# Four graph layers on one core: later small steps, a shorter split, tail products moved forward, last norms without a square root

## Chip, cores, metric

The kernel runs on one core of a Trainium2 chip. The metric is the device time of one execution in microseconds (us). The engines are TensorE (PE), VectorE (DVE), ScalarE (ACT), GpSimd (POOL) and SyncE (SP, here the queue that issues nearly all DMAs).

## The reference, cut to what matters

A graph of 3125 nodes with 128 features and 103125 edges, sorted by target, passes four layers; each is added to its input and layer-normalized over the features:

```python
x = _layernorm(x + L0(x, src, dst, edge_weight, W, b))  # relu(sum of w * (x@W)[dst] into src, + b)
x = _layernorm(x + L1(x, [src, dst], ...))   # 4-head GAT: softmax of leaky_relu(a_s[src] + a_d[dst]),
                                             # weighted sum, + bias + x@skip_W + skip_b, own layer norm
x = _layernorm(x + L2(x, Wq, Wk, Wv, Wo))    # edge attention: x + softmax(q.k) V @ Wo
x = _layernorm(x + L3(x, ...))               # two SAGE layers (mean of neighbours), sigmoid
```

## The kernel before

Nodes are padded to 3200: 25 blocks of 128. The kernel never gathers edges one by one after the front. **The front** builds two dense 3200 x 3200 matrices in DRAM from one-hot products: `f_ctd` (edge counts, bf16) and `wd` (summed edge weights, f32). All later sums are matrix products against blocks of them. PE, DVE and ACT work from instruction streams that are fixed at build time; the order in each stream is that of the program as a scheduler settles it, and a waiting instruction holds all behind it on its engine.

**Layer 0.** `add0(pool, i, accs, blocks)` loads row block `i` of `wd` (tile `cw`, line 790, on SP) and multiplies it into accumulators in PSUM (line 794). The first 20 target blocks (`Z0`) have the five banks `acc0`; their `add0` calls run inside the loop of the front as rows are written, the last two after it, with `cw` in the pool `f_zp` of three buffers. The last five blocks (`acc1`, tiles `left`) come in a second loop over all 25 row blocks: the **tail**. Between its calls stand `marks`: `scores1(g)` (transposes `turned` L909 and attention products L1087, L1091), `top`, `factors`, `values`. `end0` does relu, residual and layer norm of one bank (L801, L762 to L773).

**Layer 1** runs over `items`: four groups of target blocks (`IG`: 4, 7, 7, 7 blocks), two head pairs and 25 source blocks `c`. In each step `masks` loads a count block (`ct`, L1213) and makes two 0/1 masks, on ACT and DVE (L1225, L1226) or on DVE alone (L1219); `products` multiplies counts and masks with `vp` (L1236, L1241). `values(b)` fills `vp` for two blocks: it scales, splits f32 into three bf16 pieces (`split3`, L549 to L555) and writes a negated copy of one part (L1144). It is called four steps ahead within the first 25 steps.

All small work is put between steps with `later(k, f)`: `f` runs `k` steps on. `skips` makes the skip product of one block (L1249, read by L1250); `quotients`, then `finish1` with `first_norm`, `first_scale`, `second_norm`, `second_scale` end a group; `turns` then takes each block through `turn2`: `one` transposes (L984), `two` multiplies by `wyv` (L988), read by ACT (L989) and DVE (L990). `bound2` finds the largest norm (`highest` L942, `spread` L953). All of these write PSUM through `bank()`:

```python
    def bank():
        return spare[-1]()
        spare.append(lambda: zps.tile([P, 512], F32, name="few", tag="acc1"))   # tail, group 0
                spare.append(lambda: ap.tile([P, 512], F32, name="few"))        # groups 1 to 3
        spare.append(lambda: ss.tile([P, 512], F32, name="s"))                  # layer 2
```

In groups 1 to 3 seven of the eight banks are accumulators, and the eighth is the only one for small work.

**Layer 2** runs over two groups of targets (13 and 12 blocks) and 25 source blocks: scores (L1373), exponential (L1376), times counts (L1377), products (L1381). The first steps also hold the end of layer 1's last group, and `degrees` (a transpose L1354, ACT copy `rt` L1356, two DMAs). `finish2` normalizes: the first group in two halves between steps (`norm1`, `norm2`), the second at once by `layer_norm` with the scaling on DVE (L778).

**Layer 3** multiplies the counts with three-piece splits (`in_parts`) of its input (L1476) and of the hidden layer (L1549). At the end each of seven groups passes: sums (L1565), sigmoid on ACT (L1568), residual (L1569), `layer_norm` with square root (L767) and scaling (L773) on ACT, output DMA on SP (L1573, L1577).

## Time and profile before

| | |
|---|---|
| median of 3 runs | 1536.65 us (1534.05 to 1539.7) |
| profiled execution: time, span | 1536.56 us, 1534.5 us |
| mean PE clock granted, 1 = full | 0.979 |
| layer 1's products, first and last (L1236, L1241) | 547.8 to 961.2 us |
| layer 3's first product, PE's last product | 1261.65, 1516.07 us |
| last output DMA issued | 1528.1 us |

"L1249" is line 1249 of the kernel. A wait reads: waiting engine and line <- engine and line that released it. Busy PE is modelled from the instruction's size, so a full PE row says that PE had work, not that it ran at its peak.

### The profile page before, as it was taken

How to read it: one execution, taken by the hardware profiler on the slowest of the kernel's cores; microseconds unless marked ns; L12 is line 12 of the kernel's file. 1: busy time of each engine (PE TensorE's matmuls, PEld its weight loads, DVE VectorE, ACT ScalarE, POOL GpSimd, SP SyncE). 2: the span in 40 equal slices, each digit the busy share in tenths (PEclk: the TensorE clock that was granted, in tenths of full speed). 3: DMA queues.
4: the chain of work that ended last, by engine and by line, in shares of the span. 5: the costliest groups of instructions: out<-in, count | busy, mean ns of one | idle time of the engine just before them, and what ended most of it. 6: DMA issues, size and time to landing. Idle time of an engine off the chain costs nothing.

```text
span 1534.5 us, 35155 instructions
## 1 busy us (share of the span) xinstructions
PE 1400.5 (91%) x14871; PEld 1223.6 (80%) x14871; DVE 981.0 (64%) x1574; ACT 923.4 (60%) x1880; POOL 122.5 (8%) x136
## 2 busy tenths in 40 slices
PE   4899999999997978899989989899999989999995
PEld 3898999998997867899979889577777764458995
DVE  4999899989991389778878887544464360012005
ACT  2988778888882489878778676544474340023006
POOL 1000000000000023203311320300000000000000
PEclk9999999999999999999999999999999999999998
DMA  6387787878877623444434333332222226513551
GB/s 192 91 220 207 203 234 206 235 202 223 214 214 232 222 85 101 143 118 125 132 115 134 114 87 95 106 94 68 67 72 73 82 105 238 193 44 129 195 195 45
DMA packets 210368, 224.39 MB, mean 146 GB/s; under 512 B 72892, under 2 KB 184007, under 8 KB 209945
## 3 DMA queue, kind: packets, MB, share of 16 engines
q1 hardware_dynamic: 206344, 217.74, 48.4%
q10 hardware_dynamic: 3457, 2.35, 0.6%
q8 instruction: 118, 1.93, 0.5%
q0 software_dynamic: 400, 1.97, 0.4%
q14 instruction: 49, 0.40, 0.1%
HBM read 157.67 MB, written 64.36 MB: 145 GB/s over the span
## 4 chain that ended last, share of the span: by engine, by line
PE 40%; DVE 5%; ACT 2%; issue 1%; POOL 1%; DMA 1%; DVEq 0%; ACTq 0%; SPq 0%; POOLq 0%
PE acc L1381 9%; PE s L1373 8%; PE acc L1476 7%; PE acc L1549 6%; PE acc L1241 4%; PE acc L1236 2%; DVE cm L1226 1%; DVE nz L1260 1%; PE tr L1513 1%; PE acc L1513 1%; DMA ct<-f_ctd 1%; ACT fm L1225 1%; DVE cm L1219 0%; PE tr L1505 0%; PE acc L1505 0%
## 5 line engine op out<-in xcount | busy, mean ns | idle before, releaser
L1241 PE MATMUL acc<-vp,cm 128*128 128x198 bf16 x2500 | 344.7, 252 | 6.6 <-DVE cm L1226 4.1
L1225 ACT ACTIVATE fm<-adr,bas 128x896 bf16<-128x896 f32 (+1 forms) x320 | 286.5, 952 | 68.0 <-DVE cm L1226 63.1
L1236 PE MATMUL acc<-vp,ct 128*128 128x204 bf16 x1250 | 315.2, 256 | 10.0 <-DVE vp L1144 5.6
L1241 PEld LDWEIGHTS <-cm 128*128 128x128 bf16 x2500 | 236.0, 98 | 26.5 <-issue 10.6
L872 PE MATMUL wp<-wod,ohc 128*128 128x128 bf16 x3840 | 244.0, 219 | 8.8 <-ACT cs L877 6.6
L872 PEld LDWEIGHTS <-ohc 128*128 128x128 bf16 x3840 | 224.0, 98 | 9.8 <-issue 9.4
L833 DVE TENSOR_TENSOR wod<-ohd,w 128x4096 bf16<-128x4096 bf16 (+1 forms) x120 | 225.0, 1931 | 0.6 <-PE wp L872 0.6
L1226 DVE TENSOR_TENSOR cm<-fm,ct 128x896 bf16<-128x896 bf16 (+1 forms) x320 | 198.1, 649 | 36.1 <-PE acc L1241 14.1
L842 ACT ACTIVATE wod<-ohd,wu 128x128 bf16<-128x128 bf16 x640 | 197.0, 400 | 0.0
L1377 DVE TENSOR_TENSOR e<-e,ct 128x416 f32<-128x416 f32 (+1 forms) x175 | 110.4, 636 | 108.2 <-ACT e L1376 102.6
L1376 ACT ACTIVATE e<-s,f_nm 128x416 f32<-128x416 f32 (+1 forms) x175 | 111.5, 642 | 99.4 <-PE s L1373 94.1
L1381 PEld LDWEIGHTS acc<-self__8127,e 128*128 128x128 f32 x1250 | 148.4, 193 | 21.5 <-issue 19.7
L1373 PE MATMUL s<-yT,f_xT 128*128 128x416 f32 (+1 forms) x350 | 145.8, 552 | 4.6 <-ACT rt L1356 4.0
L1381 PE MATMUL acc<-self__8127,e 128*128 128x129 f32 x1250 | 148.7, 276 | 0.6 <-DVE e L1377 0.6
L794 PE MATMUL acc<-f_xw,cw 128*128 128x128 f32 x1000 | 118.4, 278 | 7.4 <-DMA cw<-wd 7.4
L1236 PEld LDWEIGHTS <-ct 128*128 128x128 bf16 x1250 | 122.4, 98 | 2.5 <-issue 1.5
L883 ACT COPY ws<-wp 128x512 f32<-128x512 f32 x160 | 93.6, 585 | 49.8 <-PE wp L872 48.2
L794 PEld LDWEIGHTS acc<-f_xw,cw 128*128 128x128 f32 x1000 | 115.0, 194 | 7.6 <-DMA cw<-wd 7.6
L864 PE MATMUL cp<-ohc,ohd 128*128 128x125 bf16 x1280 | 96.7, 218 | 21.1 <-ACT ws L883 17.9
L1373 PEld LDWEIGHTS s<-yT,f_xT 128*128 128x128 f32 x350 | 62.2, 191 | 57.7 <-issue 40.6
L1476 PE MATMUL acc<-ct,ip 128*128 128x512 bf16 (+1 forms) x525 | 104.9, 360 | 1.4 <-DMA ct<-f_ctd 1.4
L1549 PE MATMUL acc<-ip,ct 128*128 128x128 bf16 x1875 | 105.2, 219 | 0.0
(277 smaller groups left out, 1482.7 us busy)
## 6 DMA issues: line engine op xcount, KB each, us to landing
ct<-f_ctd SPq DMA_DIRECT2D x50, 800.0 KB
wd<-ws SPq DMA_DIRECT2D x40, 896.0 KB
ct<-f_ctd SPq DMA_DIRECT2D x150, 224.0 KB
cw<-wd SPq DMA_DIRECT2D x50, 640.0 KB
f_ctd<-cs SPq DMA_DIRECT2D x20, 1000.0 KB
ct<-f_ctd SPq DMA_DIRECT2D x25, 416.0 KB
ct<-f_ctd SPq DMA_DIRECT2D x25, 384.0 KB
cw<-wd SPq DMA_DIRECT2D x25, 320.0 KB
```

Of the source, the lines that this page charges most:

```text
L794: nc.tensor.matmul(accs[j // 4][:, j % 4, :], cw[:, j - h, :], xw[:, i, :], start=False, stop=(i == NB - 1 and (j % 4 == 3 or j == n - 1)) ...
L833: nc.vector.tensor_tensor(f[:, 0:n].rearrange("p w (a t) -> p w a t", t=2), ohd[:, 0:n].rearrange("p w (a t) -> p w a t", t=2), twos(w2[s] ...
L842: nc.scalar.activation(wod[2][:, BW + w, :], ohd[:, BW + w, :], AF.Copy, scale=w3[:, 1, at : at + 1])
L872: nc.tensor.matmul(wp[:, j, :], ohc[:, w, :], wod[s][:, w, :], start=(j == 0 and q == 0 and s == 0), stop=(j == 3 and q == 1 and s == 2), ...
L1225: nc.scalar.activation(f[:, : n * P], at, AF.Relu, bias=bas[:, c, h : h + 1], scale=UP)
L1226: nc.vector.tensor_tensor(m[:, : n * P], f[:, : n * P], ct[:, : n * P], OP.min)
L1236: nc.tensor.matmul(out_(F1, PW), ct[:, k * P : (k + 1) * P], vp[:, c, hp : hp + 2, :, 2 * F1 : V1], start=(c == 0), stop=False, skip_group ...
L1241: nc.tensor.matmul(out_(0, 2 * F1)[:, j], ms[j][:, k * P : (k + 1) * P], vp[:, c, hp + j, :, 0 : 2 * F1], start=False, stop=(c == NB - 1 a ...
L1373: nc.tensor.matmul(s[:, :m], xT[:, c * P : (c + 1) * P], yT[:, i0 * P + a : i0 * P + a + m], start=True, stop=True)
L1381: nc.tensor.matmul(acc[k // 3][:, (k % 3) * (P + 1) : (k % 3 + 1) * (P + 1)], es[q, c][:, k * P : (k + 1) * P], vo[:, c, 0 : P + 1], start ...
L1476: nc.tensor.matmul(acc[k][:, :n], ips[b // 4][:, b % 4, s, :], ct[:, c : c + n], start=(b == 0 and s == 0), stop=(b == NB - 1 and s == 2),)
L1549: nc.tensor.matmul(acc[g][:, j, :], ct[:, (b0 + j) * P : (b0 + j + 1) * P], ups[b // 4][:, b % 4, s, :], start=(b == 0 and s == 0 and j == ...
```

## The change

- `split3` writes the third piece straight from the second subtraction: an f32 tile and an ACT copy less in each split.
- `layer_norm` gets an engine for the scaling (`by`) and, with `bits`, an inverse square root from the number's bits and three Newton steps on DVE. Without `by` ACT scales, as most callers had it.
- The PSUM pool of the front closes sooner, and twelve of the 25 tail calls run ahead of the last two calls on `acc0`, six before each. `marks` come one call earlier.
- `values` negates with one POOL instruction instead of one DVE instruction per block.
- `bank(n)` takes a width. In the tail and group 0 two banks alternate; in groups 1 to 3 one tile is kept, in three slices. `turn2` takes a slice for each of its steps.
- Skips every second step instead of every step; quotients after 8 steps instead of 4; the gaps of `finish1` grow; the bound's rest comes 2 steps later.
- `degrees` at step 7 of layer 2; the second group of layer 2 is normalized in halves, with ACT scaling; layer 3's transposes and sum of degrees come a few blocks later.
- At the end POOL scales the first five groups; the last two take the Newton norm and DVE.

```diff
@@ split3
-        u = pool.tile(room or shape, F32, name=name + "2")[:, 0 : shape[1]]
-        nc.vector.tensor_tensor(u, t, o(1), OP.subtract)
-        nc.scalar.copy(o(2), u)
+        nc.vector.tensor_tensor(o(2), t, o(1), OP.subtract)
@@ layer_norm(lp, o, i, blocks, by=None, bits=False)
+        if bits:
+            v = lp.tile([P, n], F32, name="var")
+            nc.vector.tensor_scalar(v, mv[:, :, 1], EPS, None, OP.add)
+            k = lp.tile([P, n], I32, name="half")
+            nc.vector.tensor_scalar(k, v.bitcast(I32), 1, None, OP.arith_shift_right)
+            nc.vector.tensor_scalar(sd.bitcast(I32), k, -1.0, float(0x5F3759DF), OP.mult, OP.add)
+            t = lp.tile([P, n], F32, name="newton")
+            for _ in range(3):
+                nc.vector.tensor_tensor(t, sd, sd, OP.mult)
+                nc.vector.scalar_tensor_tensor(t, t, -0.5, v, OP.mult, OP.mult)
+                nc.vector.scalar_tensor_tensor(sd, t, 1.5, sd, OP.add, OP.mult)
+        else:
+            nc.vector.tensor_scalar(sd, mv[:, :, 1], EPS, None, OP.add)
+            nc.scalar.activation(sd, sd, AF.Sqrt)
+            nc.vector.reciprocal(sd, sd)
+        if by:
+            for b in range(n):
+                by.tensor_scalar(
+                    o[:, b0 + b, :], i[:, b0 + b, :], mv[:, b, 0:1], sd[:, b : b + 1], OP.subtract, OP.mult
+                )
+            return
...
@@ after the loop of the front
+    fps.close()
+    zpp = zero.enter_context(tc.tile_pool(name="f_zpp", bufs=1, space=PSUM))
...
+    early = 0
     for i in range(done, NB):
+        for _ in range(6):
+            add0(zp, early, acc1, (Z0, NB - Z0))
+            early += 1
         add0(zp, i, acc0, (0, Z0))
@@ turn2
-        t = bank()
         def one():
+            t = bank(P)
...
         def two():
-            nc.tensor.matmul(t[:, P : 3 * P], xT[:, b * P : (b + 1) * P], wyv, start=True, stop=True)
+            t = bank(2 * P)
+            nc.tensor.matmul(t[:, 0 : 2 * P], xT[:, b * P : (b + 1) * P], wyv, start=True, stop=True)
@@ bound2
-        later(1, rest)
+        later(2, rest)
@@ finish1
-            later(gap[0], lambda: turns(0))
+            later(2 * gap[0] - 1, lambda: turns(0))
...
-                later(1, two)
+                later(gap[2], two)
                 later(2, lambda: turns(j + 1))
...
-                        later(1, lambda q=q: bound2(sp, q))
+                        later(gap[2], lambda q=q: bound2(sp, q))
@@ values
-            for k in range(n):
-                nc.vector.tensor_scalar(
-                    vp[:, b + k, :, :, 2 * F1 : 3 * F1], vp[:, b + k, :, :, F1 : 2 * F1], -1.0, None, OP.mult
-                )
+            both_ = vp[:, b : b + n].rearrange("p b h s c -> p b (h s) c")
+            nc.gpsimd.tensor_scalar(both_[:, :, :, 2 * F1 : 3 * F1], both_[:, :, :, F1 : 2 * F1], -1.0, None, OP.mult)
@@ the tail
-        for i in range(NB):
-            add0(tp, i, acc1, (Z0, NB - Z0))
...
-            if i >= 13 and i % 3 == 1:
+        for i in range(early, NB):
+            add0(tp, i, acc1, (Z0, NB - Z0), NB - Z0)
...
+            if i >= NB - 2:
                 values(ready)
                 ready += 2
@@ skips, quotients, finish1's gaps
-                later(1, lambda: skips(b + 1, last))
+                later(2, lambda: skips(b + 1, last))
...
-                    later(1 if last else 3, lambda: finish1(ends[-1], g, (1, 1) if last else (1, 5)))
-            later(1 if last else 4, quotients)
+                    later(1 if last else 3, lambda: finish1(ends[-1], g, (1, 2, 1) if last else (2, 6, 3)))
+            later(1 if last else 8, quotients)
@@ groups 1 to 3
-                spare.append(lambda: ap.tile([P, 512], F32, name="few"))
+                few = ap.tile([P, 512], F32, name="few")
+                turn = [0]
+                def slices(n):
+                    turn[0] ^= n == P
+                    a = 2 * P if n > P else turn[0] * P
+                    return few[:, a : a + n]
+                spare.append(slices)
...
-            if c == (2 if g else 0) and hp == (0 if g else H - 2):
+            if c == (1 if g else 0) and hp == (0 if g else H - 2):
@@ layer 2
-                layer_norm(l2, x, r, QG[q])
+                for h in halves:
+                    norm2(norm1(cp, r, *h), x, r, *h)
...
-            if (q, c) == (0, 3):
+            if (q, c) == (0, 7):
                 degrees()
@@ layer 3
-            if 3 <= b < 17 and b % 2:
-                turned(ps, xT, *GB[(b - 3) // 2])
-            if b == 18:
+            if 6 <= b < 20 and b % 2 == 0:
+                turned(ps, xT, *GB[(b - 6) // 2])
+            if b == 19:
...
-            layer_norm(lp, x, r, (b0, n), True)
+            if g < len(GB) - 2:
+                layer_norm(lp, x, r, (b0, n), nc.gpsimd)
+            else:
+                layer_norm(lp, x, r, (b0, n), nc.vector, True)
```

## Prediction

> **What bounds the kernel now.** I read the page first, then who waited for whom on TensorE (PE), then busy time in stretches of the span, then the timeline around each PE gap.
>
> ```profile
> PE 1400.5 (91%) x14871; PEld 1223.6 (80%) x14871; DVE 981.0 (64%) x1574; ACT 923.4 (60%) x1880; POOL 122.5 (8%) x136
> ...
> PE   4899999999997978899989989899999989999995
> ```
>
> PE has work for 1400 of 1534 us and its row is rarely below 9: PE order bounds the kernel, and what a change can win is the 134 us in which PE stood still. The waits say where (columns: us in all, times, longest):
>
> ```profile
> PE few L1249 <- DVE f_xw L1250: 10.4, 7, 3.4
> PE acc L794 <- DMA cw<-wd: 7.4, 1, 7.4
> ...
> PE few L984 <- ACT f_x L975: 5.8, 2, 2.9
> PE acc L1236 <- DVE vp L1144: 5.6, 4, 2.3
> ...
> PE s L1373 <- ACT rt L1356: 4.0, 1, 4.0
> PE few L984 <- DVE self__8127 L990: 4.0, 4, 1.4
> ...
> PE few L953 <- DVE d_all L947: 2.1, 2, 1.1
> ```
>
> The tile `few` is the one spare bank of layer 1: small steps (skip product, transpose, projection) wait there for the evacuation before them. With L942 (1.3) and L988 (0.5) it costs 24.1 us. The stretches show that not all of layer 1 is PE's:
>
> ```profile
> core 0: us, PE busy (x) PEld busy (x) DVE busy (x) ACT busy (x) POOL busy (x), PEclk, DMA share, GB/s
> 547.80:599.00 51.20, 39.78 (x351) 33.71 (x352) 47.88 (x141) 48.54 (x89) 13.44 (x25) 0.93 0.29 87
> 645.00:710.00 65.00, 60.66 (x645) 58.47 (x644) 51.66 (x90) 50.20 (x67) 17.12 (x11) 0.97 0.42 120
> 1050.00:1105.00 55.00, 55.00 (x322) 41.54 (x321) 23.76 (x46) 24.09 (x47) 1.68 (x1) 1.00 0.23 70
> ```
>
> In 547.8 to 599 (first 25 steps of layer 1, with `values` between) VectorE (DVE) and ScalarE (ACT) are full and PE has 11.4 us of holes. In layer 2 (1050 on) PE has none. Last, the end:
>
> ```profile
> 1499.83 16.24 PE L1549 MATMUL acc<-ip,ct 128*128 128x128 bf16 x288
> 1524.02 1.28 ACT L767 ACT_TABLE_LOAD   x1 [0.50 <-DVE sd L766]
> 1525.97 2.03 ACT L773 ACTIVATE f_x<-f_xw,ms,sd 128x128 f32<-128x128 f32 x5 [0.35 <-DVE ms L771]
> 1528.10 0.31 SPq L1577 DMA_DIRECT2D out_dram<-f_x  x1
> ```
>
> PE is done at 1516.1, the last output is issued at 1528.1: 12 us of ACT and DVE.
>
> **What the skill says.** (1) The Trainium skill, "PSUM — Partial Sum Buffer", PSUM bank collisions: two engines are to be kept apart by bank and quadrant, not by address. If the new slices of one bank are guarded so, a slice does not let PE write while DVE reads the next one; only the later steps help. The trace of before has whole-bank tiles and can't tell. (2) "SBUF — State Buffer", Who interferes with whom, states that DVE with two SBUF inputs and GpSimd (POOL) share a port pair by an exclusive lock. The trace agrees: the 128x512 mask (L1226) takes 0.41 us, but 0.63 at 607.0 and 0.91 at 604.0, beside POOL's `nz` work. (3) "ScalarE: Activation LUTs", What ACT_TABLE_LOAD costs, gives about 1283 ns; the trace has 1.28 us at L767.
>
> **Part 1, small steps later.** One step of groups 1 to 3 is 7 x 3 products at about 0.0875 us: 1.84 us. Skips now come every second step: of the L1249 gaps (3.37, 2.30, 2.29, 1.52, 0.46, 0.26, 0.21) 1.53 + 0.46 + 0.45 remain: -8.0. The first transpose comes three steps after the scaling, not one: both gaps of 2.90 go: -5.8. The bound's L942 and its L953 (1.28, 1.03): -2.3; the other L953, in `in_range`, stays. L984 behind L990 and L988 (4.5) wait for the step just before, which still uses the bank: between 0 (bank guard) and -4.5 (slices independent); I take -2. Sum -18. Behind these waits stand PE's products, so each gap moves everything. What is late next: masks. From 603 to 961 DVE is busy 295 of 358 us, ACT 273; without 18 us DVE stands at 87%, and PE waits for `cm` 6.5 us already. I let 3 return: **-15**, ends -20 and -9. The longer chain fits: quotients at step 8, norms at 11 to 21, turns 24 to 39, bound by 43 of the next group's 50 steps.
>
> **Part 2, `degrees` at step 7.** Now the copy `rt` (L1356) stands on ACT behind a square root that waits for the second norm (ACT idle 6.1 us before L966), and holds a score bank: PE idle 4.0 at 992.2. Four steps later, and with the norm itself a step later (5.7 us, past POOL's end at 986.3), nothing holds it: **-4**, ends -4 and -1. Its two SP transfers move too; their row is read only from L1534, at 1350. The bound of the last group moves from step 22 to 24 of 25, just before the exponentials that use it. Two table loads and small work, 3.6 us, lie beside two steps of products (5.8 us): +0.5, ends 0 and +3.
>
> **Part 3, early tail products.** Twelve of the 25 calls on the last five blocks go ahead of the last two calls on the first twenty. Each is 10 PE records of 0.117: 14 us moved, none saved. What could be saved is the 7.4 us gap before 487.3. But its cause is a full DMA: share 1.08, 1.09, 1.18 in 476 to 485, while the last `wd` and `f_ctd` writes pass, and the first `cw` issued at 478.2 lands at 487.3. The early loads (12 x 320 KB) stand in the same SP queue with three buffers; the first lands at best 1.1 us earlier (320 KB less at 280 GB/s), and 6.4 MB then need 23 us, as long as PE needs for them. So the first twenty blocks end near 511, not 498, and the chain of norms, scores and factors behind them starts 13 us later, with 27 us of PE work to pass now and 23.5 after: factors at 536 against 530. If the loads get ahead of the writes, the gap goes (-7.4); if three buffers are too few, some 6 us more. I take +1.
>
> **Part 4, `values`.** The third-piece copy goes from ACT (13 x 0.63). DVE's subtraction writes bf16 instead; the 128x528 row stays at 0.71 (bounds 0.6 and 0.8: same elements). The negation goes from DVE (13 x 0.4 = 5.2) to POOL: 792 elements, between the row of 80 (0.43, L1103) and the 896 of L1022 (2.09); I take 1.3, which POOL (13 of 51 us busy) can carry. Behind it on POOL are the copies L1137, for which ACT's first piece waits. By the shared port half of DVE's gain returns: -2.6 net. Two more calls fall into the full stretch, but masks start earlier, since fewer tail products are left. -3, ends -6 and +2. Parts 3 and 4: **-2**, ends -12 and +8. Splits of layer 3 lose an ACT copy too: PE has no gap there, so 0.
>
> **Part 5, last norms.** Square root and sigmoid alternate: seven table loads from 1500 on. After, the last two groups need none, and POOL scales the other five (4 x 0.45 a group against PE's 3.3). DVE gains work: two Newton chains of 12 operations at 0.16 to 0.2 (partly interleaved, 3.5 us) and five scalings at 0.27. From the last-but-one accumulator at 1515.2 (1516.1 less the last block's 15 products of 0.056): sums 1.5, add 0.7, statistics 1.9, Newton 3.5, scaling 1.35 gives the last issue near 1524: **-4**, ends -6 and 0. Layer 2's last norm in halves: the next transfers wait for its buffers, but its first product waits for `ct` at 1261.65 anyway; 0, at worst +4. The moved transposes and sum of degrees lie in filled PE time: 0.
>
> **Sum.** -15 - 4 + 0.5 - 2 - 4 = -24.5 on the profiled execution's own 1536.56 us (span 1534.5 and 2.1 around it); the median shown, 1536.65, is the same within 0.1. Forecast **1512 us**, own range 1503 to 1523.
>
> **Rivals.** (A) The waits change their names: masks and evacuations become late at 87% DVE, and the bank is guarded whole. Then -2 for part 1, -2 for `degrees`, +2 for 3 and 4, -4 at the end: 1530.5. For it: the `cm` waits and the port lock; against it: ACT and DVE still have 60 us of slack in 603 to 961. (B) Slower, one mechanism: the loop of three load buffers at the end of the front becomes bound by latency. Sixteen tiles are 5.3 rounds; 18 us now and the 14 moved allow 6.0 us a round. It decides from 30 us lost (22.5 won elsewhere and 7.7 to be seen), 11.7 us a round; at 12.5 the time is 1549. For it: one tile took 9.1 us from issue to landing; against it: that was behind 2 MB of writes, and the later loads run at 0.8 us apart. (C) More: the early loads pass the writes (-8), all bank waits but one go (-22), `values` gives -5, `degrees` -4, the end -6: 1492. For it: DMA share is 0.57 to 0.64 in 470 to 476, and the gap is dearer than itself (PE clock granted 0.73, 0.50 and 0.63 from 482 to 491). That the diff would not do what it says is excluded but for the slices, which A holds.
>
> **Chances.** Forecast 0.63, A 0.15, B 0.07, C 0.15. A difference under about 0.5% (7.7 us) can't be told from none in this kernel. Faster: the forecast, C and a seventh of A, 0.80; same 0.13; slower 0.07. The range 1496 to 1531 takes in A and most of C.
>
> **What would show it.** Right: `few` under 9 us in PE's waits; no `rt` wait; last output about 8 us after PE's last product, without a table load between; layer 1's groups shorter by about 5 us each. The front's gap before the last two `cw` still 5 us or more. Wrong: `cm` waits over 12 us, the first product of layer 1 over 8 us later than 547.8, or POOL's scalings ending after DVE's.

## Result: slower, and the profile after

The changed kernel takes 1559.12 us (median of 4, 1555.28 to 1561.17) against 1535.38 for the kernel before beside it: ratio 1.0147, interval 1.0115 to 1.0179. The profiled execution has a span of 1555.3 us, 20.8 more than before. The page, with the two lines that answer to those shown of before:

```profile
PE 1404.0 (90%) x14871; PEld 1230.3 (79%) x14871; DVE 976.2 (63%) x1559; ACT 902.3 (58%) x1838; POOL 165.1 (11%) x169
...
PE   4899999999997877999989989899999979999994
```

PE's work is the same within 4 us. The row is a digit lower in the 14th and 16th slices (505 to 544 us, where the tail is, and 583 to 622) and two digits lower in the 33rd (1244 to 1283), between layers 2 and 3. Where the 20.8 us arose, from first and last instructions of a stage (the 2.8 us from the last group's first sum to layer 1's last product are the same in both and left out):

| stage | before | after | difference |
|---|---|---|---|
| to the end of layer 1's first 25 steps | 598.8 | 613.8 | +15.0 |
| rest of group 0 (629.2, 644.25 at its end) | 30.4 | 30.5 | 0 |
| groups 1 to 3 (to the sums at 958.05, 972.7) | 328.9 | 328.4 | -0.4 |
| layer 2, to its last product | 294.0 | 292.6 | -1.4 |
| from there to layer 3's first product | 6.8 | 13.8 | +7.0 |
| layer 3, to PE's last product | 254.3 | 253.7 | -0.6 |
| end | 18.6 | 19.8 | +1.2 |

PE's waits after (us in all, times, longest); L1008 is before's L984, L1273 its L1249, L808 its L794, L1260 and L1265 its L1236 and L1241, L1164 its L1144, L1406 its L1373; L933 is the transposes (before's L909), here those ahead of layer 3:

```profile
PE acc L1260 <- POOL vp L1164: 12.2, 9, 2.7
PE left L808 <- DMA cw<-wd: 8.6, 6, 6.6
PE few L1008 <- DVE self__8221 L1015: 8.2, 4, 3.0
PE tr L933 <- ACT f_xT L532: 7.2, 1, 7.2
PE acc L1260 <- DVE nz L1284: 7.0, 5, 2.7
...
PE few L1273 <- DVE f_xw L1274: 6.0, 6, 2.2
...
PE acc L1265 <- DVE cm L1243: 4.9, 3, 2.4
...
PE acc L808 <- DMA cw<-wd: 4.6, 2, 2.7
PE s L1406 <- ACT e L1409: 4.3, 1, 4.3
```

Of 24.1 us, `few` still has 14.8 (these two rows and 0.6 at L966). What left it came back under other names: in groups 1 to 3 all waits together are 28.8 us before (603 to 961) and 27.9 after (614 to 973). The wait of `s` for `rt` has become one for an exponential, 4.3 for 4.0. The same three stretches, each shifted with its stage:

```profile
core 0: us, PE busy (x) PEld busy (x) DVE busy (x) ACT busy (x) POOL busy (x), PEclk, DMA share, GB/s
562.40:613.80 51.40, 41.34 (x355) 37.16 (x355) 47.75 (x102) 40.53 (x72) 39.55 (x42) 0.88 0.26 76
660.00:725.00 65.00, 58.98 (x637) 56.55 (x635) 51.86 (x94) 52.01 (x69) 13.97 (x11) 1.00 0.40 118
1065.00:1120.00 55.00, 55.00 (x329) 42.87 (x328) 23.36 (x43) 24.45 (x47) 1.68 (x1) 1.00 0.24 71
```

In the first, ACT is 8 us lighter as forecast, but POOL has gone from 13.4 to 39.6 of 51.4 us, and the stretch is no shorter. The end, from the timeline (start, length):

```profile
1531.00 6.67 POOL L783 TENSOR_SCALAR f_x<-f_xw,mv,sd 128x128 f32<-128x128 f32 x8 [3.74 <-DVE t L1599]
1538.90 6.42 POOL L783 TENSOR_SCALAR f_x<-f_xw,mv,sd 128x128 f32<-128x128 f32 x8 [1.23 <-DVE sd L780]
...
1545.35 0.18 DVE L763 BATCH_NORM_AGGREGATE mv<-bs 128x2 f32<-128x6 f32 x1 [1.56 <-POOL f_x L783]
...
1549.21 0.31 SPq L1614 DMA_DIRECT2D out_dram<-f_x  x1
```

POOL scales at 0.82 us a block, and DVE's last statistics wait 1.34 and 1.56 us for it, since they write the buffers `mv` that POOL still reads. The last output goes out 13.5 us after PE's end at 1535.7; before it was 12.0.

### The profile page after: what moved, and what is told of

Read it like the earlier page. It is cut to its first block, busy times and chain, and to the rows that moved or that the text cites. A ratio compares the mean times of both kernels' runs of the same rounds, so it can differ in the third digit from the quotient of the medians.

```text
span 1555.3 us, 35152 instructions
## 1 busy us (share of the span) xinstructions
PE 1404.0 (90%) x14871; PEld 1230.3 (79%) x14871; DVE 976.2 (63%) x1559; ACT 902.3 (58%) x1838; POOL 165.1 (11%) x169
## 4 chain that ended last, share of the span: by engine, by line
PE 67%; DVE 15%; ACT 8%; DMA 4%; POOL 3%; issue 3%; ACTq 0%; SPq 0%; DVEq 0%; POOLq 0%
PE acc L1265 9%; PE acc L1414 8%; PE s L1406 8%; PE wp L886 8%; PE acc L808 7%; PE acc L1510 7%; PE acc L1583 6%; PE acc L1260 5%; DVE cm L1250 3%; ACT wod L856 3%; PE cp L878 3%; DVE wod L847 3%; DMA cw<-wd 2%; DVE ohd L838 1%; PE left L808 1%
## 5 line engine op out<-in xcount | busy, mean ns | idle before, releaser
L1265 PE MATMUL acc<-vp,cm 128*128 128x198 bf16 x2500 | 349.0, 253 | 6.1 <-DVE cm L1243 4.9
L1260 PE MATMUL acc<-vp,ct 128*128 128x204 bf16 x1250 | 319.0, 257 | 20.1 <-POOL vp L1164 12.2
L1249 ACT ACTIVATE fm<-adr,bas 128x896 bf16<-128x896 f32 (+1 forms) x320 | 286.9, 952 | 74.0 <-DVE cm L1250 73.0
L1265 PEld LDWEIGHTS <-cm 128*128 128x128 bf16 x2500 | 238.4, 99 | 36.9 <-issue 14.1
L1406 PE MATMUL s<-yT,f_xT 128*128 128x416 f32 (+1 forms) x350 | 143.8, 550 | 4.9 <-ACT e L1409 4.3
L1260 PEld LDWEIGHTS <-ct 128*128 128x128 bf16 x1250 | 123.1, 99 | 2.6 <-issue 1.3
L808 PE MATMUL acc<-f_xw,cw 128*128 128x128 f32 x1000 | 120.1, 281 | 4.6 <-DMA cw<-wd 4.6
L897 ACT COPY ws<-wp 128x512 f32<-128x512 f32 x160 | 93.5, 584 | 50.0 <-PE wp L886 48.3
L808 PEld LDWEIGHTS acc<-f_xw,cw 128*128 128x128 f32 x1000 | 116.5, 196 | 5.1 <-DMA cw<-wd 4.9
L878 PE MATMUL cp<-ohc,ohd 128*128 128x125 bf16 x1280 | 96.7, 218 | 21.0 <-ACT ws L897 17.4
L1406 PEld LDWEIGHTS s<-yT,f_xT 128*128 128x128 f32 x350 | 63.5, 191 | 54.7 <-issue 45.2
L1583 PEld LDWEIGHTS <-ct 128*128 128x128 bf16 x1875 | 104.9, 98 | 0.0
```

Source lines behind the costliest of these rows:

```text
L808: nc.tensor.matmul(accs[j // 4][:, j % 4, :], cw[:, j - h, :], xw[:, i, :], start=False, stop=(i == NB - 1 and (j % 4 == 3 or j == n - 1)) ...
L878: nc.tensor.matmul(cp[:, j, 0:KW], ohd[:, w, :], ohc[:, w, 0:KW], start=(j == 0 and q == 0), stop=(j == 3 and q == 1), skip_group_check=True,)
L1249: nc.scalar.activation(f[:, : n * P], at, AF.Relu, bias=bas[:, c, h : h + 1], scale=UP)
L1260: nc.tensor.matmul(out_(F1, PW), ct[:, k * P : (k + 1) * P], vp[:, c, hp : hp + 2, :, 2 * F1 : V1], start=(c == 0), stop=False, skip_group ...
L1265: nc.tensor.matmul(out_(0, 2 * F1)[:, j], ms[j][:, k * P : (k + 1) * P], vp[:, c, hp + j, :, 0 : 2 * F1], start=False, stop=(c == NB - 1 a ...
L1406: nc.tensor.matmul(s[:, :m], xT[:, c * P : (c + 1) * P], yT[:, i0 * P + a : i0 * P + a + m], start=True, stop=True)
```

## Experiments: which parts lost

Ratios are against the kernel before. Six runs undo parts of the change. The four runs of the changed kernel spread over 5.9 us, so a difference of 4.0 or 1.7 us in the medians is read together with the traces.

**e1_tail**: the changed kernel with the tail as before.

```diff
-        for _ in range(6):
+        for _ in range(0):
             add0(zp, early, acc1, (Z0, NB - Z0))
...
-            if i >= NB - 2:
+            if i >= 13 and i % 3 == 1:
                 values(ready)
```

> The changed kernel with the tail as it was: no early calls, the marks and the first values calls where they stood before; all other parts stay. Theory (the loss adds up by stage; the early tail products, starved by three load buffers, put the end of the first twenty blocks from 498 to 522 us and cost most of the 15 us that layer 1's first 25 steps end late): the first twenty blocks end at 498 again, the first 25 steps of layer 1 end 8 to 12 us sooner (602 to 606 instead of 613.8), whole time about 1548. Rival (the stretch of values is set by POOL's negations of 2.3 us each; the tail before it only hides): the first 25 steps end at 611 to 614 all the same, time within 3 us of the changed kernel.

Measured: 1541.72 us, ratio 1.0038 (1.0027 to 1.0049), 17.4 us less than the changed kernel. The first twenty blocks end at 499.6 instead of 522.3, layer 1's first product comes at 547.9 instead of 562.4. The early products, with the marks and the two calls of `values` that moved with them, are most of the loss.

**e2_neg**: the negation on DVE again.

```diff
-            nc.gpsimd.tensor_scalar(both_[:, :, :, 2 * F1 : 3 * F1], both_[:, :, :, F1 : 2 * F1], -1.0, None, OP.mult)
+            for k in range(n):
+                nc.vector.tensor_scalar(vp[:, b + k, :, :, 2 * F1 : 3 * F1], vp[:, b + k, :, :, F1 : 2 * F1], -1.0, None, OP.mult)
```

> The changed kernel with the negation in values on DVE, one instruction per block, as before. Theory (POOL's negation takes 2.3 us instead of 0.4 on DVE, and PE waits 12.2 us for it): the waits for POOL go, those for DVE come back at 4 to 6 us, the first 25 steps end 4 to 7 us sooner, time about 1553. Rival (DVE is full in that stretch, so its own negation of 0.4 us in 13 calls gives back 5 us): no difference within 2 us.

Measured: 1555.08, ratio 1.0119 (1.0094 to 1.0144), 4.0 less; layer 1's first 25 steps take 48.6 us instead of 51.3, 2.7 less. POOL's row in the changed kernel (us in all, mean ns):

```profile
L1164 POOL TENSOR_SCALAR vp<-vp 128x792 bf16<-128x792 bf16 x12 | 29.7, 2477 | 5.8 <-DVE vp L553 5.8
```

**e3_norm**: layer 2's last norm at once, with scaling on DVE. **e4_end**: all last norms with square root and ACT.

```diff
# e3_norm
-                for h in halves:
-                    norm2(norm1(cp, r, *h), x, r, *h)
+                layer_norm(l2, x, r, QG[q], nc.vector)
# e4_end
-            if g < len(GB) - 2:
-                layer_norm(lp, x, r, (b0, n), nc.gpsimd)
-            else:
-                layer_norm(lp, x, r, (b0, n), nc.vector, True)
+            layer_norm(lp, x, r, (b0, n))
```

> The changed kernel with the second group of layer 2 normalized at once from the pool of layer 2, DVE scaling, as before. Theory (the first count block of layer 3 waits for memory held by the small tiles of the norm in the pool that it overlays): its transfer is issued 2 us after the last product of layer 2, not 9.4, layer 3 starts 6 to 7 us sooner, time about 1552. Rival (the longer gap comes from ACT, which now scales and copies one after the other): the transfer is early but PE still starts late, at most 2 us gained.

> The changed kernel with the last norms as before: square root and scaling on ACT for all seven groups. Theory (POOL takes 0.82 us for a scaling, 3.3 us a group, as much as PE needs, and DVE waits for the tiles that POOL still reads): from PE's last product to the last output 12 us instead of 13.5, time 1 to 2 us shorter. Rival (the Newton norm does pay, POOL is beside it): 2 to 4 us longer.

Measured: e3_norm 1553.43 (1.0109, 1.0092 to 1.0126), 5.7 less, and layer 3's first product 6.0 us after layer 2's last, not 13.8. e4_end 1557.44 (1.0141, 1.0124 to 1.0158), 1.7 less, and the last output goes out 12.0 us after PE's end, not 13.5.

**e5_four** undoes all four. **e9_three** undoes all but POOL's negation.

> All four undone at once: old tail, negation on DVE, old last norm of layer 2, old last norms at the end; what stays of the change are the later small steps and slices, the copy less per split, the moved degrees and the moved transposes of layer 3. Theory (the four single effects, -17.4, -4.0, -5.7 and -1.7 us, mostly add up): 1530 to 1534 us, 2 to 6 below the kernel before. Rival (negation on POOL cost only where the tail was late, and the later steps lose time themselves): 1536 to 1541.

> As the kernel with all four undone, but with the negation on POOL. Theory (the wait for POOL costs 4 us wherever the tail is): 3 to 5 us slower than with all four undone. Rival (with the old tail the first values calls run beside tail products, so POOL keeps up): equal within 1.5 us, or faster, since DVE is freed of 5 us.

Measured: 1533.85 (0.9982, 0.9973 to 0.9991) and 1533.49 (0.9979, 0.997 to 0.9987). So tail, norm and end (17.4, 5.7, 1.7) add up to the 25 us between e5_four and the changed kernel. The negation costs only with the early tail. It is not covered in e9_three: PE waits 8.1 us for POOL's `vp` in the first 25 steps, where it waits 3.0 us for DVE's in e5_four (548 to 598 us, e9_three first):

```profile
PE acc L1260 <- POOL vp L1164: 8.1, 5, 2.9
```

```profile
PE acc L1262 <- DVE vp L1164: 3.0, 4, 1.2
```

But its other waits there are shorter, and the steps take 48.9 us against 48.3. Why the early tail makes the negation dearer, no run shows.

**e6_four_newton**: e5_four with the Newton norm and DVE for the last two groups.

```diff
-            layer_norm(lp, x, r, (b0, n))
+            if g < len(GB) - 2:
+                layer_norm(lp, x, r, (b0, n))
+            else:
+                layer_norm(lp, x, r, (b0, n), nc.vector, True)
```

> The kernel with early tail products, POOL negation and halved last norm of layer 2 all undone, and of the last norms only POOL undone: ACT with square root for the first five groups, Newton and DVE for the last two. Beside e5_four (1533.85, square root and ACT for all seven) it tells the worth of Newton alone. Theory 1 (the end was lost to POOL's scaling of 0.82 us and to what waits for its buffers): the last output goes out 8 to 9 us after PE's last product, not 12, and the time is 1530 to 1531.5. Theory 2 (twelve DVE instructions of 0.16 us in a chain cost what the square root with its table loads costs): 1533 to 1535.

Measured: 1534.03 (0.9981, 0.9975 to 0.9988), the same as e5_four. The last output still goes out 12.0 us after PE's end. Without POOL, Newton neither gains nor loses: theory 2.

**e8_small6**: the changed kernel, but the tiles `cw` of the front are six of five blocks, not three of ten.

```diff
-        for h in range(0, n, 10):
-            m = min(10, n - h)
-            cw = pool.tile([P, w, P], F32, name="cw")[:, 0:m]
+        for h in range(0, n, 5):
+            m = min(5, n - h)
+            cw = pool.tile([P, 5, P], F32, name="cw")[:, 0:m]
...
-    zp = front.enter_context(tc.tile_pool(name="f_zp", bufs=3))
+    zp = front.enter_context(tc.tile_pool(name="f_zp", bufs=6))
```

> The changed kernel with the front's three load buffers of ten blocks as six of five blocks: the same memory, each load half as large. Theory (early products starve because three loads in flight are too few for the time from issue to landing): the gaps before the cw products from 480 to 515 shrink from 13 us to 7 or less, the first twenty blocks end at 512 to 516 instead of 522, time 6 to 12 us shorter. Rival (it is the bandwidth behind the last writes, not the number of loads): the end of the first twenty blocks moves by less than 3 us.

Measured: 1549.22 (1.0086, 1.0071 to 1.0102), 9.9 less. PE's timeline at the end of the front, first the changed kernel, then e8_small6 (the bracket is PE's idle time before):

```profile
486.34 5.25 PE L808 MATMUL left<-f_xw,cw 128*128 128x128 f32 x30 [6.59 <-DMA cw<-wd]
...
498.32 4.95 PE L808 MATMUL acc<-f_xw,cw 128*128 128x128 f32 x40 [1.83 <-DMA cw<-wd]
...
514.83 7.43 PE L808 MATMUL acc<-f_xw,cw 128*128 128x128 f32 x40 [2.74 <-DMA cw<-wd]
```

```profile
486.70 8.96 PE L808 MATMUL left<-f_xw,cw 128*128 128x128 f32 x60 [6.36 <-DMA cw<-wd]
495.49 4.63 PE L808 MATMUL acc<-f_xw,cw 128*128 128x128 f32 x40
...
506.66 4.63 PE L808 MATMUL acc<-f_xw,cw 128*128 128x128 f32 x40
```

The first gap stays in both, as in before (7.37 us) and e1_tail (7.12): neither order nor size of the loads that were tried removes it. The gaps after it, 6.5 us, and the slow last forty products (7.43 us for 4.63) go with six smaller loads; whether their number or their size does it is not separated. What is left of the tail's loss, 7.5 us, remains with the tail products moved: the first twenty blocks end at 511.3, layer 1 starts 6.5 us late.

**f_l2pool**: the changed kernel with the small tiles of layer 2's last norm in another pool.

```diff
-                    norm2(norm1(cp, r, *h), x, r, *h)
+                    norm2(norm1(l2, r, *h), x, r, *h)
```

> The changed kernel, with the small tiles of layer 2's last norm in the pool f_lp2 instead of f_cp2; the scaling stays on ACT in two halves. Theory 1 (layer 3's first count loads wait because their buffers lie over those small tiles, which ACT reads until its last scaling): the first L1501 is issued some 7 us earlier, and layer 3's first product comes 5 to 7 us earlier than the 13.8 us after layer 2's last one: 1553.5. Theory 2 (the scaling on ACT itself holds, since the first split stands behind it on ACT and takes 4.7 us for 12 blocks): the loads go out early, but the first product stays within 2 us of where it was, and the time at 1558 to 1560.

Measured: 1549.99 (1.0087, 1.0072 to 1.0103), 9.1 less, of which 7.7 lie between the layers (6.1 us instead of 13.8). SP's waits around the first count loads of layer 3, changed kernel and f_l2pool:

```profile
SPq L1501 <- DVE ms L997: 21.5, 1, 21.5
...
SPq L1501 <- ACT f_x L999: 4.1, 1, 4.1
```

```profile
SPq L1501 <- DVE f_xw L1477: 18.0, 1, 18.0
```

The first load is issued at 1277.41 in the one, 9.4 us after layer 2's last product, and at 1269.19 in the other, 1.8 us after its last. Halves and ACT cost nothing; the memory of the small tiles did. Their pool `f_cp2` lies where layer 3's count buffers come, so the loads waited for the last scaling.

## Experiments: where the gain of the later steps went

**p1_putoff**: the kernel before with Part 1 alone, its slices and its gaps.

```diff
-                later(1, lambda: skips(b + 1, last))
+                later(2, lambda: skips(b + 1, last))
...
-                    later(1 if last else 3, lambda: finish1(ends[-1], g, (1, 1) if last else (1, 5)))
+                    later(1 if last else 3, lambda: finish1(ends[-1], g, (1, 2, 1) if last else (2, 6, 3)))
-            later(1 if last else 4, quotients)
+            later(1 if last else 8, quotients)
```

> The kernel before with the later small steps alone: bank by width, two banks in turn and slices of one bank, skips every second step, quotients after 8, the longer gaps. Theory (groups 1 to 3 took 328.9 us before and 328.5 in the changed kernel, since DVE and ACT set their length and the waits only change names): within 3 us of the kernel before, groups 1 to 3 within 1.5 us. Rival (the forecast's: each gap on the spare bank moves all of PE): 9 to 15 us faster.

Measured: 1534.87 (0.9989, 0.998 to 0.9997); groups 1 to 3 take 330.8 us against 328.9. Nothing was won. Two timelines of it show why, DVE first, then PE:

```profile
654.79 0.87 DVE L961 BATCH_NORM_STATS2 bs<-f_xw 128x6 f32<-128x128 f32 x4 [5.33 <-POOL f_xw L1025]
655.58 0.61 DVE L1233 TENSOR_TENSOR cm<-fm,ct 128x896 bf16<-128x896 bf16 x1
656.11 0.28 DVE L1257 TENSOR_TENSOR f_xw<-few,f_both 128x128 f32<-128x128 f32 x1
...
656.45 0.49 PE L1256 MATMUL few<-f_l_swt,f_xT 128*128 128x128 f32 x2 [3.23 <-DVE f_xw L1257]
```

DVE stands 5.33 us at the statistics of the second norm, waiting for the three POOL additions of `first_scale`. A mask and a skip's evacuation are queued behind, and PE waits 3.23 us for that evacuation. The Trainium skill, "PSUM — Partial Sum Buffer", Engine vs sequencer instructions, calls the VectorE queue strict FIFO; the trace agrees, and this is what it costs. DVE was free by occupancy and blocked by order.

**d_before, d_putoff**: before and p1_putoff with masks of 128 columns. With other numbers the kernel runs a slow second path behind the dense one, so their times, 6871.45 (4.4705, 4.4636 to 4.4773) and 6862.71 (4.465, 4.4581 to 4.4718), say nothing; the trace of layer 1 comes ahead of that path and is read.

```diff
-                m = mp.tile([P, 7 * P], BF16, name="cm")
+                m = ct
...
-                        m[:, : n * P], at, nas[:, c, h : h + 1], ct[:, : n * P], OP.is_gt, OP.mult
+                        ct[:, :P], at[:, :P], nas[:, c, h : h + 1], ct[:, :P], OP.is_gt, OP.mult
...
-                    nc.vector.tensor_tensor(m[:, : n * P], f[:, : n * P], ct[:, : n * P], OP.min)
+                    nc.vector.tensor_tensor(ct[:, :P], f[:, :P], ct[:, :P], OP.min)
```

> The kernel before, with layer 1's masks made on the first 128 columns of a count block alone, in place (the other columns keep their counts: that part of the computation is left out). VectorE (DVE) then has some 180 us less of 295 in 603 to 961, while the products of TensorE (PE), the ACT instructions and the small steps stay as they are. Theory 1 (DVE's backlog at the group boundaries is what PE waits for, whatever the tile is called): the waits of few behind L1250 (10.4 us) and of acc behind nz and cm (8 us) go for the greater part, groups 1 to 3 take 329 us less some 12, and the waits of one step (L984 behind ACT L975, 5.8, behind L990, 4.0) stay. Theory 2 (the one small bank is what costs, and DVE does not): few stays above 18 of its 24 us and the groups take 325 to 329.

> The kernel before with the later small steps and the slices alone, and with the same masks of 128 columns as its companion without them (the rest of the masks is left out). Theory 1 (in p1_putoff the win of the later steps was taken back by DVE's backlog): with DVE relieved, few falls under 4 us, and the run is 5 to 10 us shorter than its companion. Theory 2 (the bank is guarded whole, so a slice waits as the bank did): few L984 behind L991 stays at 6 to 8 us and the run is within 3 us of its companion. Theory 3 (also the waits of before were DVE's lateness): both runs lose them, and they differ by under 3 us with few under 6 us in both.

Measured: in groups 1 to 3 DVE is busy 140 and 127 us instead of 269, and they take 322.0 and 321.8 us instead of 328.9. `few` keeps 20.7 and 17.4 us. So no theory of d_before held whole; in d_putoff the second did for layer 1 (6.6 us behind L991, 0.2 us from its companion). DVE's load is worth 7 us of these groups, but it is not what takes back the later steps' gain, for they gain nothing even without it. In d_putoff DVE stands at the statistics as before, 24.7 us with layer 2's.

**g_before, g_four, g_four_last** put the second norm later in the program.

```diff
# g_before
-finish1(ends[-1], g, (1, 1) if last else (1, 5))
+finish1(ends[-1], g, (1, 1) if last else (1, 9))
# g_four, on e5_four
-finish1(ends[-1], g, (1, 2, 1) if last else (2, 6, 3))
+finish1(ends[-1], g, (1, 2, 1) if last else (2, 10, 3))
# g_four_last, on g_four
-finish1(ends[-1], g, (1, 2, 1) if last else (2, 10, 3))
+finish1(ends[-1], g, (1, 5, 1) if last else (2, 10, 3))
-                later(2, lambda: turns(j + 1))
+                later(1 if gap[2] == 1 else 2, lambda: turns(j + 1))
```

> The kernel before, with the second norm of groups 0 to 2 nine steps after the three POOL additions (L1022 to L1024), not five. In the profile of before, DVE stands at that norm's statistics (L961) for POOL three times, 12.1 us in all, with skip evacuations and masks queued behind. Theory 1 (this head of DVE's queue is what several waits of few and cm are): the three waits of L961 go, few falls from 24 to 13 to 17 us, groups 1 to 3 take 322 to 326 us, not 329, and the time is 1530 to 1533. Theory 2 (DVE's standing is covered by masks made ahead; the one bank costs): few stays at 21 to 24 and the time within 2 us of 1536.5.

> The changed kernel with early tail products, POOL negation, halves and last norms undone (e5_four, 1533.85), and the second norm ten steps after the POOL additions, not six. In e5_four DVE stands 18.5 us there, in three times up to 6.7. Theory 1 (the later small steps of the change win what was forecast, and the norm's wait for POOL takes it back): groups 1 to 3 shorten by 8 to 14 us, few and cm fall under 10 us together, time 1520 to 1526. Theory 2 (lateness of POOL counts little): 1531 to 1534. In between (other places of DVE's queue, as the 21 sums of nz and the masks, take over): 1527 to 1531.

> As g_four, and in the last group of layer 1 the second norm comes five steps after the POOL additions (not two) and the transposes follow in every step (not every second). In e5_four ACT stands 6 us at that norm's square root, and PE 4.3 us for the exponential behind it. Theory 1 (that wait is POOL's lateness again): the wait of s behind the exponential goes, 3 to 4.5 us less than g_four. Theory 2 (the bunched transposes take it back from layer 2's banks): within 1.5 us of g_four.

Measured: 1538.23 (1.0009, 1.0001 to 1.0018), 1533.84 (0.9978, 0.9968 to 0.9989) and 1532.64 (0.997, 0.9958 to 0.9982), which would fit theory 2. But the wait that was to go is still there. DVE's waits (603 to 1100 us) of before, then g_before:

```profile
DVE bs L961 <- POOL f_xw L1024: 18.9, 4, 6.7
```

```profile
DVE bs L961 <- POOL f_xw L1024: 18.9, 4, 6.7
```

The edit did not do what it says. In DVE's stream, as the traces have it, the second norm's statistics of groups 1 and 2 stand 10 masks behind the first norm's in before and still 10 in g_before; in e5_four they stand 12 masks behind, and still 12 in g_four. The scheduler had put them there all the same, it seems by when it holds their inputs for ready. So `later` did not order these statistics on DVE, though it orders PE's small steps. These three runs tell nothing of the wait, only that it wasn't moved.

**h_before, h_four** hold the statistics in place: they may be issued only behind the mask (in layer 2, the product with the counts) of the step that the program puts them in.

```diff
-            keep["b"] = norm1(sp, r, i0, n)
+            with tc.issue_after(newest[0].ins):
+                keep["b"] = norm1(sp, r, i0, n)
...
-                    nc.vector.tensor_tensor(m[:, : n * P], f[:, : n * P], ct[:, : n * P], OP.min)
+                    newest[0] = nc.vector.tensor_tensor(m[:, : n * P], f[:, : n * P], ct[:, : n * P], OP.min)
# the other mask form and the product with counts likewise; gaps:
# h_before
+finish1(ends[-1], g, (1, 1) if last else (2, 7))
# h_four, on e5_four; turns in every step in the last group
+finish1(ends[-1], g, (1, 4, 1) if last else (2, 8, 3))
```

> As g_before, but the statistics of the second norm are now held in DVE's stream behind the masks of the step in which the program puts them (an order, no wait); the norm's gaps are 2 and 7 steps instead of 1 and 5. g_before moved them in the program alone, and DVE still stood the same 12.1 us for POOL at L961: the planner had left them after 9 masks in the stream. Held, they stand after 15 to 19 masks. Theory 1 (DVE's standing there costs PE time): the wait of L961 for POOL goes to under 2 us, groups 1 to 3 take 322 to 326 us and the time is 1529 to 1533. Theory 2 (the masks made ahead cover it, other places set the pace): the wait goes and the time stays within 2 us of 1536.5.

> As g_four, with the statistics of the second norm held behind the masks of their step (22 to 26 masks after the first norm, not 9), and in the last group behind the exponentials of theirs, with four steps for POOL and a transpose in every step. In e5_four and g_four DVE stood 18.5 us for POOL in layer 1 and 6.7 us in layer 2, and ACT 6.1 us behind the latter. Theory 1 (this standing took back the forecast gain of the later small steps and of the degrees): the waits go, groups 1 to 3 take 318 to 323 us, the 4.3 us of s behind the exponential goes, time 1520 to 1526. Theory 2 (it does not count): the waits go, time 1531 to 1534.

Measured: **1525.73** (0.9931, 0.9917 to 0.9945) and **1515.75** (0.9867, 0.9852 to 0.9882). No row of `bs` behind the additions L1025 or L1050 is left in DVE's waits; only short ones for L1284 (2.2 us) and L1310 (4.2) are. In the traces the statistics now stand 18 and 28 masks behind. Theory 1 holds, in both runs by more than expected. The page of h_four, and its waits from 603 to 1010:

```profile
PE 1397.1 (92%) x14871; PEld 1222.0 (81%) x14871; DVE 991.2 (65%) x1574; ACT 908.7 (60%) x1853; POOL 123.7 (8%) x136
...
PE   4899999999997987999999999999999989999995
```

```profile
PE few L1014 <- ACT f_xT L532: 4.0, 2, 2.0
PE few L1277 <- DVE f_xw L1278: 3.8, 5, 1.3
PE acc L1264 <- DVE nz L1288: 3.4, 2, 2.5
PE few L1014 <- DVE f_xT L534: 2.6, 1, 2.6
PE acc L1269 <- DVE cm L1254: 1.4, 4, 0.5
```

Groups 1 to 3 take 316.9 us, 12.0 less than before (h_before: 322.5), and all of PE's waits in them come to 16.5 us (before 28.8, h_before 23.2); layer 2 286.9 against 294.0 (h_before: 288.7), without a wait for `rt` or the exponential. The stretch from 629 to 945 us, before, e5_four and h_four:

```profile
629.00:945.00 316.00, 288.52 (x3067) 277.54 (x3067) 261.39 (x480) 244.29 (x320) 75.46 (x54) 0.98 0.41 119
```

```profile
629.00:945.00 316.00, 292.55 (x3092) 280.77 (x3090) 256.96 (x476) 243.81 (x318) 72.25 (x54) 0.97 0.41 117
```

```profile
629.00:945.00 316.00, 301.61 (x3221) 291.32 (x3221) 276.34 (x489) 247.77 (x322) 74.97 (x54) 0.98 0.42 120
```

In the same 316 us h_four has done 3221 PE instructions and before 3067, and PE is busy 301.6 us, not 288.5. h_four is the fastest version of all, better than both kernels.

**i_after**: the changed kernel whole with h_four's edits.

> The changed kernel whole (early tail products, POOL negation, halves in f_cp2 and POOL scaling kept), with the edits of h_four: the second norm's statistics held in DVE's stream at their step, and the last group's gap and turns as there. Theory 1 (the loss at the tail, at layer 3's start and at the end is apart from the norm's wait): as e5_four to h_four, 18 us less than the changed kernel's 1559.12, 1539 to 1543. Theory 2 (the two overlap, since the later start of layer 1 or POOL's extra work in it covered part of the wait): 1545 to 1552.

Measured: 1540.36 (1.0023, 1.0015 to 1.0031), 18.8 less than the changed kernel; e5_four to h_four was 18.1. So the gain of the held norm and the loss of the other parts add up, within 0.7 us.

## Why the prediction was wrong

The forecast was 1512, the result 1559: 47 us apart. For Parts 1 and 2 the sum had -18.5 with the added small work; e5_four, which keeps them and the shorter split, is 2.7 us under the 1536.56 that the sum starts from: 16 us. For the rest it had -6, and the runs show +25: 31 us.

**Part 1, later small steps (-15; measured about 0).** The failed step is "The longer chain fits: quotients at step 8, norms at 11 to 21": it took `later` to move work in every engine's stream. At the ends of groups 0, 1 and 2 the quotients, put 4 steps (8 masks) later in the program, stand 6, 10 and 10 masks behind the sums in DVE's stream, where they stood 6, 8 and 8. After group 1 DVE reached the second norm 28.7 us behind the sums (30.0 before), and POOL was done only after 35.4 (34.2). So DVE stood there longer than before. Its waits, 603 to 1100 us, changed kernel:

```profile
DVE bs L985 <- POOL f_xw L1049: 25.3, 4, 6.7
```

I had read the gaps of L1249 and L984 as a matter of the one bank. Three of them, 3.37 us at 653.5 and 2.90 at 774.7 and 885.2, come behind a standing DVE (until 651.4, 768.6 and 879.0). The prediction read PE's waits and not DVE's; nor did the rival of late masks name that cause. The size was wrong too: with the norm held, groups 1 to 3 take 322.5 us without the later steps (h_before) and 316.9 with them (h_four). The later steps, with one step more for the norm, are then worth 5.6 us, not 15; the other 6.4 of the 12.0 come from the held norm. On the slices rival A held, that they do not overlap: at 709.50 a transpose into one slice waits 2.99 us for L1015, which reads another slice. Whether the bank is guarded, or the one tile of which the slices are cut, this does not tell.

**Part 2, `degrees` (-4; layer 2 is 1.4 us shorter in the changed kernel, 0.2 in e5_four).** `rt` no longer waits, but the square root that held it still stands in ACT's stream behind the norm that waits for POOL (DVE idle 6.7 us, ACT 6.1), and the exponential behind it now makes PE wait 4.3 us. I had named POOL's end at 986.3 as what frees it, and taken one step of program for 5.7 us of time. The failed step is "with the norm itself a step later". h_four holds the norm back, and layer 2 is 7.1 us shorter than before; 5.3 of them h_before has too, with `degrees` where it stood.

**Part 3, early products (+1; measured +17.4).** Two errors. The failed step is the chain behind the first twenty blocks, "factors at 536 against 530". By the prediction's own numbers (13 us later, 3.5 us less to pass) the difference was 9.5 us, not 6, and the sum took +1 for the whole part. In e8_small6, where the first twenty blocks end at 511.3 as I had it, the exponentials of `factors` come at 545.2 instead of 530.4: the way there, up to the first product into `few`, takes 29.8 us against 30.5 and is hardly shorter. From those exponentials to layer 1's first product PE had 121 tail products to do in before, and has none in e8_small6 (columns as above, before first):

```profile
530.40:547.80 17.40, 16.11 (x146) 15.94 (x145) 11.88 (x30) 8.46 (x17) 4.75 (x17) 1.00 0.52 163
```

```profile
545.20:554.30 9.10, 2.90 (x10) 2.17 (x11) 9.10 (x27) 8.57 (x19) 7.20 (x14) 0.52 0.11 32
```

So layer 1 starts only 6.5 us late and not 14.8, but PE stands 6.2 of these 9.1 us: by the traces, the products that were moved forward had covered this chain. The second step is the one that the prediction left out of its sum: "if three buffers are too few, some 6 us more" came true, with 6.5 us of gaps and PE at half clock behind them; six smaller loads win back 9.9 us. The rival of three buffers had the right mechanism, with too high a threshold. The Trainium skill, "TensorE: Matmul & The Clock Gate", What's actually happening, has the clock halved after an idle window of about 3.4 us; the trace agrees for the 6.59 us gap (0.52 granted from 485 to 490), and shows it with one of 2.74 too (0.59 from 514 to 522), where the page's window alone would not give it.

**Part 4, `values` (-3; the split gained, the negation lost).** With the copy less per split layer 1's first 25 steps take 48.3 us in e5_four; in p1_putoff, without it, they take 50.9 (before 51.0). The mis-sized term is POOL's negation: 1.3 us taken, 2.48 measured, over the upper bound of 2.09. Interpolating by elements between two other POOL rows failed; this one reads and writes a strided view of three-part rows, but no run tells whether the stride is the reason. With the early tail it cost 4.0 us by the medians and 2.7 in these steps, with the old tail 0.6 in them (e9_three).

**Part 5, last norms (-4; measured +1.7, in the trace +1.5) and layer 2's norm ("0, at worst +4"; measured +7.0 between the layers).** POOL's scaling takes 0.82 us, not 0.45; four are as long as PE's 3.3 us for a group, and DVE's statistics wait for its buffers. Newton alone is worth 0 (e6_four_newton). In layer 2 I priced ACT's time, where the memory under the small tiles decided: the transfer waited for the last reader of what lay there before. Undone (e3_norm) or moved to another pool (f_l2pool), layer 3's first product comes 7.8 and 7.7 us sooner.

Of the signs given, the front's gap stayed, as said. `few` was to be under 9 us (14.8), the last output 8 us after PE (13.5), and the groups shorter by 5 us each (0.1 on average; one after the other they changed by 0.0, +3.9 and -4.4). Of the signs of being wrong one came: layer 1's first product was 14.6 us late.

## To carry to other kernels

Before costing a step that is put off, find the engine's own stream: look who stands at the head of the queue, for whom, and what is queued behind it, even on an engine that is busy two thirds of the time; and check after building that the moved instruction stands elsewhere in that stream. Before moving work forward, look what it covers where it stands. A wait that is taken off one bank or buffer comes back under another name as long as the producer behind it stands still: add up all waits of the stage, not those of one tile. Small tiles belong in a pool whose memory nothing that is loaded next will need.

## What the runs showed of the hardware

One effect is larger than in the prediction's reading (0.41 to 0.91 us): DVE beside POOL. In h_four the masks are made while POOL adds (759.4 to 766.8), where DVE stood before:

```profile
759.39 3.08 DVE L1247 SCALAR_TENSOR_TENSOR cm<-adr,nas,ct 128x896 bf16<-128x896 f32 x1 [0.22 <-PE acc L1269]
762.39 4.94 DVE L1254 TENSOR_TENSOR cm<-fm,ct 128x896 bf16<-128x896 bf16 x2
767.25 0.28 DVE L1278 TENSOR_TENSOR f_xw<-few,f_both 128x128 f32<-128x128 f32 x1
767.45 1.14 DVE L1254 TENSOR_TENSOR cm<-fm,ct 128x896 bf16<-128x896 bf16 x2
```

A mask of 1.14 us (the length of L1247 elsewhere in this stream) takes 3.08, two others that take 1.14 together take 4.94, and POOL's additions 2.09 to 2.81 instead of 2.08. The three masks end at 762.47, 764.89 and 767.33, each 0.5 to 1.0 us behind the end of one addition (761.52, 764.41 and 766.84): the two engines take turns. That fits the exclusive port pair of the Trainium skill, "SBUF — State Buffer", Who interferes with whom, which the prediction used. Slow masks still beat none: three were made in the time in which DVE had stood.
